# An LSTM with a residual in float32 on one core: weight rows regrouped over 128 partitions, scales per row and chunk, two scalings moved to GpSimd, and wider x products

## The chip, the cores and the metric

The kernel runs on one core of a Trainium2 chip. A core has TensorE (PE, with a weight-load stage shown as PEld), VectorE (DVE), ScalarE (ACT), GpSimd (POOL) and SyncE (SP), each with an instruction queue of its own; they hand work to each other through semaphores. The metric is the device time of one execution in microseconds, the median over several runs. A profile is taken of one execution and has a time of its own.

## The reference

```python
# x: (16, 512, 512), h0: (16, 512), Wx and Wh: (512, 2048), b: (2048,), all float32
xW = einsum('ntd,dg->ntg', x, Wx) + b
def step(carry, xw_t):
    prev_h, prev_c = carry
    a = xw_t + prev_h @ Wh
    i, f, o = sigmoid(a[:, :H]), sigmoid(a[:, H:2*H]), sigmoid(a[:, 2*H:3*H])
    g = tanh(a[:, 3*H:])
    next_c = f * prev_c + i * g
    next_h = o * tanh(next_c)
    return (next_h, next_c), next_h
hs = scan(step, (h0, zeros), xW over time)
return x + hs                       # (16, 512, 512)
```

N = 16 sequences, T = 512 steps, D = H = 512 inputs and units. Each step needs the state of the step before it, so 512 steps follow one another; the products x @ Wx don't depend on the state. The function's arguments are called x, cond_1024 (the h0 above), L0_cond_Wx, L0_cond_Wh and L0_cond_b in the profile.

## The kernel before

**Layout.** The 128 partitions are 4 blocks `j` of 32 (`NJ = 4`, `Q = 32`). For gate sums, block `j` holds the units 128j to 128j+127 along the free axis, and its 32 partitions are rows: 16 sequences twice. Inputs come in pairs of steps (`S2 = 2`, index `q` or `p`), eight steps to a load (`XB = 8`, index `s`, `load_xs`, L138). The DVE's transpose works in squares of 32 x 32, so it turns a gate tile with sequences on partitions into one with units on partitions: partition 32j + k then holds the units 128j + 32c + k for the four chunks `c`. The rows of the weights lie the same way: `load_w` copies, for chunk `c` and block `j`, 32 rows from 128j + 32c on (16 transfers of 256 KB for each of Wh and Wx). The 512 units are treated in two halves, a and b (`h` = 0 and 1, chunks 0, 1 and 2, 3), so that one half's products can run while the other half's elementwise work does.

**Float32 products from float16 parts.** Wh is multiplied by a power of two and split once, at the start, into three float16 parts `wq[0..2]`: the rounded value (L381, ACT), the residual `r1` (L383, DVE) rounded (L384, ACT), and the residual of that, `r2` (L386, DVE), times 4096 (L387, ACT); eight halves of chunks, in `split`. The power of two comes from the largest absolute value of a partition over all four chunks (L360 reduces, L363 to L375 small operations on one column). S is its scale for the output gate, RS and RS2 those for the weights, RSL what undoes S. All of Wh must have landed before the first split, as the scale comes from all of it.

The state is split too: `p1` (L276) writes the rounded product os * tanh(c) into a slot of `parts`, `h` (L270) the float32 value to `hist`, `copy` (L280, ACT), `p2` (L282), `rem` (L286) and `p2r` (L290) the other slots. `os` is the output gate times S (`scale`, L258, ACT: a column as scale).

**One step on PE.** The order is written out in a string. Each `qikh` is a group of eight products (128 x 256, float16) of part `i`, the state's half `k` and the gates' half `h`; four blocks `j` run side by side in the array's columns. Three parts by four combinations make 96 products (`products`, L180). Behind them come `x0` to `x3`, 32 float32 products of 256 columns (`project`, L157), which make the x products two pairs ahead. `seed` (L167, ACT) writes the x sum into a gates bank before a step's products add to it. The first step uses float32 Wh itself (`first_products`, L193).

```python
STEP_PE = "q3aa q3ab q1ab q1aa q2aa q3ba q1ba q2ba q2bb q1bb q2ab q3bb x0 x1 x2 x3"
```

**One step elsewhere.** The order of the elementwise operations is written out too, and no scheduler changes it:

```python
STEP = (
    "turn_a turno_a fold_a tanh_a foldo_a sig_a turn_b sigo_a scale_a mix_a fold_b "
    "tanh_b cell_a ctanh_a turno_b foldo_b sig_b p1_a sigo_b h_a copy_a mix_b p2_a "
    "scale_b cell_b rem_a ctanh_b p2r_a p1_b h_b copy_b p2_b rem_b p2r_b"
)
```

`turn` and `turno` (L216, DVE) transpose a half's gates out of PSUM, `fold` and `foldo` (L223, DVE) add the low-order rows divided by 4096 to the high-order ones, `tanh` (L250), `sig` (L252), `sigo` (L256) and `ctanh` (L268) are ACT's functions, `mix` (L260, one operation for f * c and i * g) and `cell` (L266) DVE's. A step's last operation, `p2r_b`, completes the state's half b, which `q2ba` and `q2bb` of the next step need. In step 0, p1 also waits for memsets of `parts` on POOL.

Every second step ACT undoes the scale for the output (`unscale`, L299: 128 x 128), DVE turns it (L308), POOL adds x (L309), and every eight steps SP issues eight stores (L315) and eight loads of x. Intermediate tiles of a step have two buffers (`work`, `state`), so that an operation writes where that of two steps ago wrote.

**The start.** SP issues the 16 loads of Wh, four of h0, eight of x, then 16 of Wx; ACT's queue issues the bias. Then the scales, the eight splits, the x products of four steps and the seeds; the eight PSUM banks are zeroed by products of a float32 zero row.

## Time and profile before

| | |
|---|---|
| median of 3 runs | 2321.29 us (2321.03 to 2322.24) |
| the profiled execution | 2319.52 us |
| its span | 2317.7 us |
| granted TensorE clock | 0.997 of full speed |
| instructions | 153,753 |
| DMA | 52.13 MB, 22 GB/s on average |
| Wh's loads: issue to landing | 7.6 us (median of 16) |
| Wx's loads: issue to landing | 8.7 us (median of 16) |

The page lists, for each engine, busy time, its share of the span and the number of instructions. Its chain follows the work that ended last back from the end, step by step to what released each instruction, and gives shares by engine. The windows give the same busy figures for a chosen stretch, with the number of instructions in brackets. The timeline has one instruction to a line: start in us, duration in us, engine, line, operation, what it writes and reads with shapes (partitions x elements), and a count. The listing of events has, for each, its duration in ns and its start. A group's row in the list of costly groups has the busy time, the mean duration of one in ns, and the idle time of the engine before them with what ended most of it; PE's groups show durations with overlap in them.

### The profile page before, as it was taken

To read this page: it belongs to the slowest core of one execution; us is meant where nothing else is said; L and a number is where in the kernel's file an instruction comes from. 1 tells how busy PE (TensorE), PEld (TensorE's weight loads), DVE (VectorE), ACT (ScalarE), POOL (GpSimd) and SP (SyncE) were. 2 spreads that over 40 slices of the span, in tenths; PEclk is the share of its full clock that TensorE was granted. 3 is DMA by queue.
4 is the path that set the end of the run, shared out by engine and by line. 5 is a ranking of instruction groups with operands and counts; after the bars stand their busy time and mean duration, and the time that the engine had idled before them with its cause. 6 is when DMAs were issued, how large, how long until landed. Compare 5 with 4: busy or idle time off the path is not lost.

```text
span 2317.7 us, 153753 instructions
## 1 busy us (share of the span) xinstructions
PE 2263.9 (98%) x65584; PEld 1862.2 (80%) x65584; DVE 1958.8 (85%) x11808; ACT 1791.7 (77%) x7704; POOL 117.6 (5%) x264
## 2 busy tenths in 40 slices
PE   4899999999999999999999999999999999999997
PEld 1788888888888888888888888888888888888886
DVE  4788888888888888888888888888888888888887
ACT  3777777777777777777777777777777777777776
POOL 0000000000000000000000000000000000000000
PEclk9999999999999999999999999999999999999999
DMA  7000000000000000000000000000000000000000
GB/s 164 8 18 23 16 20 23 16 20 22 14 22 23 13 23 22 13 23 22 13 22 21 15 23 18 17 23 18 18 22 18 18 23 15 21 23 15 21 18 13
DMA packets 84907, 52.13 MB, mean 22 GB/s; under 512 B 17088, under 2 KB 83200, under 8 KB 83200
## 3 DMA queue, kind: packets, MB, share of 16 engines
q1 hardware_dynamic: 83584, 42.04, 7.9%
q8 instruction: 516, 8.45, 1.6%
q14 instruction: 167, 1.37, 0.2%
q10 hardware_dynamic: 640, 0.26, 0.1%
HBM read 25.46 MB, written 16.78 MB: 18 GB/s over the span
## 4 chain that ended last, share of the span: by engine, by line
PE 96%; DVE 1%; DMA 1%; ACT 1%; issue 0%; ACTq 0%; SPq 0%; POOLq 0%; POOL 0%; DVEq 0%
PE gates L180 58%; PE xb L157 38%; DMA wh_sb<-in_L_cond_Wh_dram 1%; DVE r L383 0%; ACT wq L381 0%; ACT wq L387 0%; PE gates L193 0%; ACT wq L384 0%; DMA bias<-in_L_cond_b_dram 0%; ACTq L334 0%; DVE gt L216 0%; DMA xs<-in_x_dram 0%; SPq L138 0%; DVE r L386 0%; ACT xb L147 0%
## 5 line engine op out<-in xcount | busy, mean ns | idle before, releaser
L180 PE MATMUL gates<-wq,parts 128*32 128x256 f16 x49056 | 1452.1, 273 | 5.3 <-DVE parts L276 4.2
L180 PEld LDWEIGHTS <-parts 128*32 128x32 f16 x49056 | 1306.3, 96 | 155.3 <-DVE parts L276 5.8
L157 PE MATMUL xb<-wx_sb,xT 128*32 128x256 f32 x16384 | 987.0, 380 | 27.1 <-DMA wx_sb<-in_L_cond_Wx_dram 27.1
L157 PEld LDWEIGHTS xb<-wx_sb,xT 128*32 128x32 f32 x16384 | 554.0, 110 | 270.3 <-ACT wq L381 20.2
L216 DVE STREAM_TRANSPOSE gt<-gates 128x192 f32<-128x192 f32 x1024 | 392.1, 383 | 237.0 <-PE gates L180 176.2
L250 ACT ACTIVATE gc<-pre 128x32 f32<-128x32 f32 x1022 | 235.0, 230 | 327.8 <-DVE pre L223 314.8
L167 ACT ACTIVATE gates<-xb,mask 128x256 f32<-128x256 f32 x1024 | 451.5, 441 | 0.0
L258 ACT ACTIVATE os<-so,sc 128x32 f32<-128x32 f32 x1024 | 329.1, 321 | 16.7
L280 ACT COPY parts<-parts 128x32 f16<-128x32 f16 x1022 | 214.5, 210 | 132.1 <-DVE parts L276 132.1
L223 DVE SCALAR_TENSOR_TENSOR pre<-gt 128x96 f32<-128x96 f32 x1024 | 254.2, 248 | 0.0
L252 ACT ACTIVATE sif<-pre 128x64 f32<-128x64 f32 x1024 | 245.5, 240 | 0.0
L216 DVE STREAM_TRANSPOSE gto<-gates 128x64 f32<-128x64 f32 x1024 | 230.3, 225 | 0.0
L309 POOL TENSOR_TENSOR ob<-hb,xs 128x128 f32<-128x128 f32 x256 | 116.6, 456 | 2193.6 <-DVE hb L308 1927.7
L256 ACT ACTIVATE so<-preo 128x32 f32<-128x32 f32 x1024 | 226.7, 221 | 0.0
L290 DVE SCALAR_TENSOR_TENSOR parts<-rem,parts 128x32 f16<-128x32 f32 x1022 | 196.6, 192 | 35.5
L268 ACT ACTIVATE tch<-gc 128x32 f32<-128x32 f32 x1024 | 226.3, 221 | 0.1
L223 DVE SCALAR_TENSOR_TENSOR preo<-gto 128x32 f32<-128x32 f32 x1024 | 193.0, 188 | 17.5
L282 DVE SCALAR_TENSOR_TENSOR parts<-parts,hist 128x32 f16<-128x32 f16 x1022 | 192.8, 189 | 17.7
L260 DVE TENSOR_TENSOR pr<-sif,gc 128x64 f32<-128x64 f32 x1022 | 205.6, 201 | 0.0
L276 DVE TENSOR_TENSOR parts<-os,tch 128x32 f16<-128x32 f32 x1022 | 196.7, 192 | 0.0
L266 DVE TENSOR_TENSOR gc<-pr 128x32 f32<-128x32 f32 x1024 | 192.9, 188 | 0.0
L270 DVE SCALAR_TENSOR_TENSOR hist<-os,tch 128x32 f32<-128x32 f32 x1024 | 189.6, 185 | 0.3 <-ACT tch L268 0.3
(42 smaller groups left out, 685.4 us busy)
## 6 DMA issues: line engine op xcount, KB each, us to landing
xs<-in_x_dram SPq DMA_DIRECT2D x512, 32.0 KB, 2.6
out_dram<-ob SPq DMA_DIRECT2D x512, 32.0 KB, 2.5
wh_sb<-in_L_cond_Wh_dram SPq DMA_DIRECT2D x16, 256.0 KB, 7.6
wx_sb<-in_L_cond_Wx_dram SPq DMA_DIRECT2D x16, 256.0 KB, 8.7
bias<-in_L_cond_b_dram ACTq DMA_DIRECT2D x8, 32.0 KB, 3.3
h_in<-in_cond_dram SPq DMA_DIRECT2D x4, 8.0 KB, 6.9
```

The lines of the kernel that those rows point to most:

```text
L157: nc.tensor.matmul(xb[q % NXB][j * Q : (j + 1) * Q, (1 - e) * GU : (2 - e) * GU], lhsT=xT[q][:, c], rhs=wx_j[:, c, e, j], start=False, sto ...
L167: nc.scalar.mul(gates[h][t % 2][:, :GU].rearrange("p (g u) -> p g u", g=G), xb[t // 2 % NXB].rearrange("p (g h u) -> p h g u", g=G, h=2)[: ...
L180: nc.tensor.matmul(g[j * Q : (j + 1) * Q, :GU], lhsT=a[:, cc, k * N : (k + 2) * N], rhs=wq_j[i - 1][:, 2 * kh + cc, h, j], start=False, st ...
L216: nc.vector.transpose(gt.rearrange("p b m -> p (b m)"), gates[h][t % 2][:, b0 * Q : b1 * Q])
L223: nc.vector.scalar_tensor_tensor(pre.rearrange("p g (c n) -> p (g c) n", c=2), gt[:, :, (1 - t % 2) * N : (2 - t % 2) * N], 1.0 / LO, gt[: ...
L250: nc.scalar.activation(gc[h][:, 0], v["pre", h][:, 0], AF.Tanh)
L252: nc.scalar.activation(new("sif", t, h, [P, 2, 2 * N]), v["pre", h][:, 1:3], AF.Sigmoid)
L256: nc.scalar.activation(new("so", t, h, [P, 2 * N]), v["preo", h][:, 0], AF.Sigmoid)
L258: nc.scalar.mul(new("os", t, h, [P, 2 * N]), v["so", h], S)
L260: nc.vector.tensor_tensor(new("pr", t, h, [P, 2, 2 * N]), v["sif", h], gc[h], ALU.mult)
L268: nc.scalar.activation(new("tch", t, h, [P, 2 * N]), gc[h][:, 1], AF.Tanh)
L280: nc.scalar.copy(slots(t, h, 2), slots(t, h, 0))
```

## The change

The unit on partition p in chunk c becomes 4p + c, where p is the partition of the weights. Each of Wh's chunks is then one transfer over 128 partitions (2,048 columns a row), and Wx comes in eight of 1,024 columns. The transposes of x and h0 read with a step of four elements, the residual's addition reads and writes with one, and so do the splits of Wh, whose parts have the unit's position modulo 4 as an axis; halves a and b of the gates are positions 0, 1 and 2, 3. The gate products read runs of 32 columns in place of 64.

Each partition and chunk gets a scale of its own, from that row of Wh alone (on odd chunks from the sum of the absolute values, an accumulation on ACT; on even ones from the largest, on DVE). So `scales(c)` and the splits of chunk c need only chunk c. The splits are written out as five parts `part(n, k)` in an interleaved order; the last part of every third half moves from ACT to POOL. As the scale now differs by chunk, `scale` is a product with a small tile on POOL, and `unscale` becomes `descale`, a product with a tile on POOL too.

An x product has 512 columns for 256, 16 for 32 in a step. The first loads of x move to ACT's queue, those of h0 and the bias to POOL's; the zero row is float16; the last pair of steps is stored apart from the three before it, on two queues (`put`).

Lines of the changed kernel that the prediction names: L269 `cell`, L279 `p1`, L289 `rem`, L293 `p2r`.

```diff
-STEP_PE = "q3aa q3ab q1ab q1aa q2aa q3ba q1ba q2ba q2bb q1bb q2ab q3bb x0 x1 x2 x3"
+STEP_PE = "q3aa q3ab q1ab q1aa q2aa q3ba q1ba q2ba q2bb q1bb q2ab q3bb x0 x1"
...
-    wq = [const.tile([P, NK, G * H], HP, tag=f"wq{i}", name=f"wq{i}") for i in range(3)]
-    wx_j = wx_sb.rearrange("p c (e g j w) -> p c e j g w", e=2, g=2, j=NJ)
-    wh_j = wh_sb.rearrange("p c (e g j h u) -> p c e h j g u", e=2, g=2, j=NJ, h=2)
-    wq_j = [w.rearrange("p c (g j h u) -> p c h j g u", g=G, j=NJ, h=2) for w in wq]
+    wq = [const.tile([P, NK, NK, G * P], HP, tag=f"wq{i}", name=f"wq{i}") for i in range(3)]
+    wx_j = wx_sb.rearrange("p c (g j w) -> p c j g w", g=G, j=NJ)
+    wh_j = wh_sb.rearrange("p c (e g j u h d) -> p c e h j g d u", e=2, g=2, j=NJ, u=Q, h=2)
+    wq_j = [w.rearrange("p c (h d) (g j u) -> p c h j g d u", h=2, g=G, j=NJ) for w in wq]
...
-    zero = const.tile([1, G * P], FP, tag="zero", name="zero")
+    zero = const.tile([1, G * P], HP, tag="zero", name="zero")
+    ones = const.tile([P, Q], FP, tag="ones", name="ones")
     amax = const.tile([P, NK], FP, tag="amax", name="amax")
-    top = const.tile([P, 1], FP, tag="top", name="top")
...
-    sc = const.tile([P, 5], FP, tag="sc", name="sc")
-    S, RS, RS2, RSL = (sc[:, i : i + 1] for i in range(4))
+    bits = const.tile([P, NK, 2], FP, tag="bits", name="bits")
+    sc = const.tile([P, NK, 4], FP, tag="sc", name="sc")
+    scale = const.tile([P, NK, N], FP, tag="scale", name="scale")
+    unscale = const.tile([P, NK, Q], FP, tag="unscale", name="unscale")
...
-    def load_w(dst, w, c):
-        for j in range(NJ):
-            r0 = j * P + c * Q
-            nc.sync.dma_start(out=dst[j * Q : (j + 1) * Q, c], in_=w[r0 : r0 + Q])
+    def rows(w):
+        return w.rearrange("(p c) f -> p c f", c=NK)
     xs = {}
-    def load_xs(s):
+    def load_xs(s, dma=nc.sync):
         xs[s] = xsp.tile([P, XP, P], FP, tag="xs", name=f"xs_{s}")
         for j in range(NJ):
             for r in range(S2):
                 p0 = j * Q + r * N
-                nc.sync.dma_start(
+                dma.dma_start(
                     out=xs[s][p0 : p0 + N],
                     in_=x[:, s * XB + r : (s + 1) * XB : S2, j * P : (j + 1) * P],
                 )
...
     def turn_x(q):
         s, i = divmod(q, XP)
         xT[q] = xtp.tile([P, NK, Q], FP, tag="xT", name=f"xT_{q}")
-        nc.vector.transpose(xT[q].rearrange("p c m -> p (c m)"), xs[s][:, i])
-    def project(q, c, e):
+        nc.vector.transpose(xT[q], xs[s][:, i].rearrange("p (u c) -> p c u", c=NK))
+    def project(q, c):
         for j in range(NJ):
             nc.tensor.matmul(
-                xb[q % NXB][j * Q : (j + 1) * Q, (1 - e) * GU : (2 - e) * GU],
+                xb[q % NXB][j * Q : (j + 1) * Q],
                 lhsT=xT[q][:, c],
-                rhs=wx_j[:, c, e, j],
+                rhs=wx_j[:, c, j],
...
     def seed(t, h):
         nc.scalar.mul(
-            gates[h][t % 2][:, :GU].rearrange("p (g u) -> p g u", g=G),
-            xb[t // 2 % NXB].rearrange("p (g h u) -> p h g u", g=G, h=2)[:, h],
+            gates[h][t % 2][:, :GU].rearrange("p (g d u) -> p g d u", g=G, d=2),
+            xb[t // 2 % NXB].rearrange("p (g u h d) -> p h g d u", g=G, h=2, d=2)[:, h],
             mask[:, t % 2 : t % 2 + 1],
         )
...
         elif op == "scale":
-            nc.scalar.mul(new("os", t, h, [P, 2 * N]), v["so", h], S)
+            nc.gpsimd.tensor_tensor(
+                two(new("os", t, h, [P, 2 * N])),
+                two(v["so", h]),
+                scale[:, 2 * h : 2 * h + 2],
+                ALU.mult,
+            )
...
-    def unscale(p):
-        hs[p] = work.tile([P, P], FP, tag="hs", name=f"hs_{p}")
-        nc.scalar.mul(
-            hs[p], hist[p // XP][:, p % XP].rearrange("p c m -> p (c m)"), RSL
-        )
+    def descale(p):
+        hs[p] = work.tile([P, NK, Q], FP, tag="hs", name=f"hs_{p}")
+        nc.gpsimd.tensor_tensor(hs[p], hist[p // XP][:, p % XP], unscale, ALU.mult)
+    def put(s, i0, i1, dmas):
+        for j in range(NJ):
+            for r in range(S2):
+                p0 = j * Q + r * N
+                dmas[r % len(dmas)].dma_start(
+                    out=out[:, s * XB + S2 * i0 + r : s * XB + S2 * i1 : S2, j * P : (j + 1) * P],
+                    in_=ob[s][p0 : p0 + N, i0:i1],
+                )
     def residual(p):
         s, i = divmod(p, XP)
         if i == 0:
             ob[s] = outp.tile([P, XP, P], FP, tag="ob", name=f"ob_{s}")
         hb = work.tile([P, P], FP, tag="hb", name=f"hb_{p}")
-        nc.vector.transpose(hb, hs[p])
-        nc.gpsimd.tensor_tensor(ob[s][:, i], hb, xs[s][:, i], ALU.add)
-        if i < XP - 1:
-            return
...
+        nc.gpsimd.tensor_tensor(
+            ob[s][:, i].rearrange("p (u c) -> p u c", c=NK),
+            hb.rearrange("p (c u) -> p u c", c=NK),
+            xs[s][:, i].rearrange("p (u c) -> p u c", c=NK),
+            ALU.add,
+        )
+        if p == NP - 1:
+            put(s, i, i + 1, [nc.sync, nc.scalar])
+        elif p == NP - 2:
+            put(s, 0, i + 1, [nc.sync])
+        elif i == XP - 1:
+            put(s, 0, XP, [nc.sync])
...
-    nc.vector.memset(zero, 0.0)
+    for c in range(NK):
+        nc.sync.dma_start(out=wh_sb[:, c], in_=rows(wh)[:, c])
+    load_xs(0, nc.scalar)
     nc.vector.memset(h_in, 0.0)
-    for c in range(NK):
-        load_w(wh_sb, wh, c)
     for j in range(NJ):
-        nc.sync.dma_start(out=h_in[j * Q : j * Q + N], in_=h0[:, j * P : (j + 1) * P])
-    load_xs(0)
+        nc.gpsimd.dma_start(out=h_in[j * Q : j * Q + N], in_=h0[:, j * P : (j + 1) * P])
     b_j = b.rearrange("(o e g j w) -> j e o g w", o=1, e=2, g=2, j=NJ)
     for j in range(NJ):
         for e in range(2):
-            nc.scalar.dma_start(
+            nc.gpsimd.dma_start(
                 out=bias[j * Q : (j + 1) * Q, (1 - e) * GU : (2 - e) * GU].rearrange(
                     "p (g w) -> p g w", g=2
                 ),
                 in_=b_j[j, e].broadcast_to([Q, 2, P]),
             )
     for c in range(NK):
-        load_w(wx_sb, wx, c)
+        for e in range(2):
+            nc.sync.dma_start(
+                out=wx_sb[:, c, (1 - e) * GH : (2 - e) * GH],
+                in_=rows(wx)[:, c, e * GH : (e + 1) * GH],
+            )
     load_xs(1)
+    nc.vector.memset(zero, 0.0)
+    nc.vector.memset(ones, 1.0)
...
-    nc.scalar.activation(warm, zero[:, 0:1], AF.Sigmoid)
+    nc.scalar.activation(warm, ones[0:1, 0:1], AF.Sigmoid)
...
-    for c in range(NK):
-        nc.vector.tensor_reduce(
-            amax[:, c : c + 1], wh_sb[:, c], mybir.AxisListType.X, ALU.max, apply_absolute_value=True
+    def scales(c):
+        top = amax[:, c : c + 1]
+        if c % 2:
+            junk = tmp.tile([P, G * H], HP, tag="junk", name=f"junk_{c}", bufs=1)
+            nc.scalar.activation(junk, wh_sb[:, c], AF.Abs, accum_out=top)
+        else:
+            nc.vector.tensor_reduce(
+                top, wh_sb[:, c], mybir.AxisListType.X, ALU.max, apply_absolute_value=True
+            )
+        e, inv = bits[:, c, 0:1], bits[:, c, 1:2]
+        S, RS, RS2, RSL = (sc[:, c, i : i + 1] for i in range(4))
+        nc.vector.tensor_scalar(
+            inv.bitcast(I32), top.bitcast(I32), EXP, EXP, ALU.bitwise_and, ALU.bitwise_xor
         )
-    nc.vector.tensor_reduce(top, amax, mybir.AxisListType.X, ALU.max)
-    nc.vector.tensor_scalar(
-        bits[:, 0:1].bitcast(I32), top.bitcast(I32), EXP, None, ALU.bitwise_and
-    )
-    nc.vector.tensor_scalar(
-        bits[:, 1:2].bitcast(I32), top.bitcast(I32), EXP, EXP, ALU.bitwise_and, ALU.bitwise_xor
-    )
-    nc.vector.tensor_scalar(sc[:, 4:5], bits[:, 1:2], 2.0**13, 1.0, ALU.mult, ALU.min)
...
-    def split(c, e):
...
-    nc.vector.transpose(hT0.rearrange("p c m -> p (c m)"), h_in)
+        nc.vector.tensor_scalar(e.bitcast(I32), top.bitcast(I32), EXP, None, ALU.bitwise_and)
+        nc.vector.tensor_scalar(RS2, inv, 2.0**12, 0.5, ALU.mult, ALU.min)
+        nc.vector.tensor_scalar(RS, inv, 2.0**13, 1.0, ALU.mult, ALU.min)
+        nc.vector.tensor_scalar(S, e, 2.0**-14, 1.0, ALU.mult, ALU.max)
+        nc.vector.tensor_scalar(RSL, RS, 1.0 / LO, None, ALU.mult)
+        nc.gpsimd.tensor_scalar(scale[:, c], ones[:, :N], S, None, ALU.mult)
+        nc.gpsimd.tensor_scalar(unscale[:, c], ones, RSL, None, ALU.mult)
+    r1, r2 = {}, {}
+    def part(n, k):
+        c, e = divmod(n, 2)
+        w = wh_sb[:, c, e * GH : (e + 1) * GH].rearrange("p (a d) -> p d a", d=NK)
+        f = [q[:, c, :, (1 - e) * GU : (2 - e) * GU] for q in wq]
+        RS, RS2 = sc[:, c, 1:2], sc[:, c, 2:3]
+        if k == 0:
+            nc.scalar.mul(f[0], w, RS2)
+        elif k == 1:
+            r1[n] = tmp.tile([P, NK, GU], FP, tag="r1", name=f"r1_{n}")
+            nc.vector.scalar_tensor_tensor(r1[n], w, RS, f[0], ALU.mult, ALU.subtract)
+        elif k == 2:
+            nc.scalar.copy(f[1], r1[n])
+        elif k == 3:
+            r2[n] = tmp.tile([P, NK, GU], FP, tag="r2", name=f"r2_{n}")
+            nc.vector.tensor_tensor(r2[n], r1[n], f[1], ALU.subtract)
+        elif n % 3 == 2:
+            nc.gpsimd.tensor_scalar(f[2], r2[n], LO, None, ALU.mult)
+        else:
+            nc.scalar.mul(f[2], r2[n], LO)
     for q in range(2):
         turn_x(q)
-    last = None
+    scales(0)
+    part(0, 0)
+    part(0, 1)
+    nc.vector.transpose(hT0, h_in.rearrange("p (u c) -> p c u", c=NK))
+    for q in range(2):
+        put_bias(q)
+    for n in range(2 * NK):
+        if n % 2 and n + 1 < 2 * NK:
+            scales((n + 1) // 2)
+        if n + 1 < 2 * NK:
+            part(n + 1, 0)
+        part(n, 2)
+        if n + 1 < 2 * NK:
+            part(n + 1, 1)
+        part(n, 3)
+        part(n, 4)
     for c in range(NK):
-        for e in range(2):
-            todo = split(c, e)
-            if last:
-                last()
-            last = todo
-            if (c, e) == (0, 0):
-                for q in range(2):
-                    put_bias(q)
-    last()
-    for q in range(2):
-        for c in range(NK):
-            for e in range(2):
-                project(q, c, e)
+        for q in range(2):
+            project(q, c)
     for t in range(2):
         for h in range(2):
             seed(t, h)
...
         for op in STEP_PE.split():
             if op[0] == "x":
-                i = int(op[1:])
                 if q < NP:
-                    project(q, 2 * half + i // 2, i % 2)
+                    project(q, 2 * half + int(op[1:]))
             elif t:
                 products(t, int(op[1]), "ab".index(op[2]), "ab".index(op[3]))
             elif op[1] == "3":
...
         if t + 2 < T:
             seed(t + 2, 0)
         if t % 2:
-            unscale(t // 2)
+            descale(t // 2)
             if q + 1 < NP:
                 turn_x(q + 1)
         else:
```

## The prediction

> **What bounds the kernel now.** I read the page's busy shares, then its chain, then the windows, and last the timeline of single steps. The page says TensorE:
>
> ```profile
> PE 2263.9 (98%) x65584; PEld 1862.2 (80%) x65584; DVE 1958.8 (85%) x11808; ACT 1791.7 (77%) x7704; POOL 117.6 (5%) x264
> ...
> PE 96%; DVE 1%; DMA 1%; ACT 1%; issue 0%; ACTq 0%; SPq 0%; POOLq 0%; POOL 0%; DVEq 0%
> ```
>
> The windows say otherwise. The first holds two steps of mid-loop; the second about one of the last steps, which have no x products left.
>
> ```profile
> core 0: us, PE busy (x) PEld busy (x) DVE busy (x) ACT busy (x) POOL busy (x), PEclk, DMA share, GB/s
> 996.00:1004.72 8.72, 8.72 (x264) 7.17 (x260) 7.60 (x48) 6.90 (x31) 0.46 (x1) 1.00 0.03 6
> 2300.00:2304.40 4.40, 2.98 (x96) 2.32 (x96) 3.57 (x24) 3.38 (x16) 0.00 (x0) 1.00 0.00 0
> ```
>
> Without its 32 x products PE is busy 2.98 us of a step, and the step still takes 4.36 (products start at 2300.75 and 2305.11). So the step is set by a loop through PE, DVE and ACT, and the x products only fill it. In the single matmul records 24 groups of four f16 products take 109 ns each and 8 groups of x products 216 ns: 4.34 us of PE work in a median step of 4.362. The PE stands 0.02 us below the loop, a coincidence that hides which of the two decides.
>
> The loop in one step, from half b's turn to its last part:
>
> ```profile
> 1003.15 0.38 DVE L216 STREAM_TRANSPOSE gt<-gates 128x192 f32<-128x192 f32 x1
> ...
> 1003.57 0.26 DVE L223 SCALAR_TENSOR_TENSOR pre<-gt 128x96 f32<-128x96 f32 x1
> ...
> 1003.86 0.23 ACT L250 ACTIVATE gc<-pre 128x32 f32<-128x32 f32 x1
> 1004.00 0.21 ACT L268 ACTIVATE tch<-gc 128x32 f32<-128x32 f32 x1
> ...
> 1004.24 0.19 DVE L276 TENSOR_TENSOR parts<-os,tch 128x32 f16<-128x32 f32 x1
> ...
> 1004.71 0.19 DVE L266 TENSOR_TENSOR gc<-pr 128x32 f32<-128x32 f32 x1
> ...
> 1004.93 0.23 ACT L268 ACTIVATE tch<-gc 128x32 f32<-128x32 f32 x1
> ...
> 1005.19 0.19 DVE L276 TENSOR_TENSOR parts<-os,tch 128x32 f16<-128x32 f32 x1
> ...
> 1005.85 0.19 DVE L290 SCALAR_TENSOR_TENSOR parts<-rem,parts 128x32 f16<-128x32 f32 x1
> ```
>
> Read ends against starts: fold_b ends 1003.83 and tanh_b starts 0.03 later; ctanh_a follows tanh_b at ACT's issue distance of 0.135; p1_a starts 0.03 after ctanh_a ends, then mix_b, cell_b, ctanh_b, p1_b, the parts. From turn_b to the start of p2r_b is 2.70 us; its 0.19, 0.15 to q2ba, ten groups of products (1.00) and 0.32 until turn_b can read the gates make 4.36. Each nanosecond on these hand-overs returns in 511 steps.
>
> **The change, part by part.**
>
> *Waits.* An instruction carries one semaphore wait; a second stands before it as an EVENT_SEMAPHORE, and the engine's sequencer decodes the instruction only after that. The profile has this case at p1, in step 0 alone, where p1 also waits for POOL's memsets:
>
> ```profile
> L276 DVEq EVENT_SEMAPHORE  x2: 21/21/21, 72.4 to 73.4; - x2
> ```
>
> ```profile
> 71.29 0.38 DVE L216 STREAM_TRANSPOSE gt<-gates 128x192 f32<-128x192 f32 x1
> ...
> 72.13 0.21 ACT L268 ACTIVATE tch<-gc 128x32 f32<-128x32 f32 x1
> ...
> 72.45 0.19 DVE L276 TENSOR_TENSOR parts<-os,tch 128x32 f16<-128x32 f32 x1
> ...
> 74.13 0.20 DVE L290 SCALAR_TENSOR_TENSOR parts<-rem,parts 128x32 f16<-128x32 f32 x1
> ```
>
> There ctanh to p1 takes 0.10 us instead of 0.03, and turn_b to p2r_b 2.84 instead of 2.70: 0.14 us for two, 69 ns each. In the changed program every p1 waits for ACT (tch) and POOL (os), with the late ACT wait on the EVENT_SEMAPHORE: 1,032 DVE instructions with two waits, 5 before. And on ACT, where the removed scale was the only instruction to wait on ACT's own semaphore and so covered for the rest, tanh, sigo, ctanh and the seeds now carry that wait (sigo one on POOL) beside the old one: 4,083 instructions with two waits, 1 before. The own wait points two steps back and is always met, but the late DVE wait was moved to the EVENT_SEMAPHORE. ACT's one-semaphore events take 17 ns, DVE's 21, so I scale 69 x 17/21 = 56 ns; the least is the 17 ns itself, the most DVE's 69. On the loop lie tanh_b, ctanh_b and two p1. ctanh_a is held by tanh_b + 0.135 (1004.05) later than by cell_a + 0.09 (1004.02), so its event hides. Sum: 2 x 69 + 2 x 56 = 250 ns a step (172 to 276), x 511 = +127.8 us (+88 to +141). Queued behind each waiting instruction is the rest of that engine's step, and the weight load of q2ba waits for its end. The two seed events and sigo's cost nothing: ACT idles 0.48 to 0.71 us before tanh_a.
>
> *Scale and descale on POOL.* ACT loses two L258 (321 ns) a step and an hs (390) every second: worth nothing, as ctanh_b starts 0.03 after cell_b anyway. os_a can start 0.08 after sigo_a (POOL's distance behind hb), at 1003.57; p1_a needs it at 1004.24, with the events at 1004.37. Its price lies between a quarter of the 456 ns of L309 (four times the elements) and all of it: done by 1004.03, hidden; os_b (1004.71 to 1005.17, needed 1005.44) too. What covers descale and the reordered residual is a POOL idle 2,193 us.
>
> *POOL beside DVE.* 183 of the turns of gates ran beside L309 at the same 383 ns, but a turn has one PSUM input. No DVE operation with two SBUF inputs, as nearly all others on the loop are, ever overlapped a POOL one here. Floor 0; ceiling, if each POOL operation pushes the loop back for its whole length, 2 x 0.114 + 0.456/2 = 0.456 us a step. I take 0.06, half of one os, near the floor where the only rows are: +31 us (0 to +233). The Trainium skill speaks against this part: "SBUF — State Buffer", "Who interferes with whom", says that a VectorE instruction with two SBUF inputs and a GpSimd instruction that reads SBUF exclude each other for a whole instruction. By that rule the ceiling would be the better guess, some +202 us on my sum; by the turn rows, -31.
>
> *x products.* 16 of 512 columns for 32 of 256 save one overhead per group: 216 - 213 = 2.5 ns x 4 = 10 ns a step of PE. On a PE that is no longer the limit: 0 (at most -5 us). Products read 32-element runs instead of 64; ten groups lie on the loop, unknown, taken as 0.
>
> *Start.* Before: L381 starts at 28.24, after the whole of Wh; the last L387 ends at 65.00, first products 65.38. After: chunk 0 lands about 10.9 (as the first four loads here; then 4.65 us per MB). Reduce 2.29 and scalars 1.1 (27.24 to 28.24 before) put the first split at 14.5. ACT's order is p0 of the next half (1.15), p2 (1.04), then p4 (1.05), which waits for DVE's p3 (1.23): 4.47 a half, 3.3 where POOL does p4. Six and two make 33.4; the scales of chunks 1 and 3 add 3.1 each (Abs, some 2.0 by L381's rate, and scalars), chunk 2's 3.5, bias copies 1.1, hand-overs 1: ready at 60, so -5 us. The order wins less than landing early promises, since loads end at 25 and the split is what lasts. wx is in by 43, hidden. Faster loads would bring 3 more. L381 and L383 now read Wh with a step of four elements; no row shows that, and doubling these 16 adds 17. Range -8 to +12. The same page's section on the DMA port swizzle notes 16-byte lines, with a penalty for each new one; every such read is a new line, so by that rule the start would be nearer +12.
>
> *End.* Eight stores issue 0.47 apart on SP; four each on two queues save 1.8. POOL's descale for ACT's 0.40: +0.1. Together -1.7.
>
> **Sum.** The profiled execution took 2319.5 (span 2317.7, 1.8 around it), 1.8 below the median 2321.3. 2319.5 + 127.8 + 31 - 5 - 1.7 = 2471.6; say 2472, or 2473 on the median's footing.
>
> **Rivals.**
> - *The split waits cost nothing* (faster): if they passed before the late semaphore, or the PE really set the step, the loop keeps 4.36 and start and end leave 2319.5 - 6.7 = 2313. For it: 98% PE. Against: step 0 at p1, and the last steps. It decides if the events and collisions together stay under 6.7/511 = 13 ns a step. 7%.
> - *POOL and DVE exclude each other* on the loop, at 0.3 us a step instead of 0.06: 2319.5 + 127.8 + 153 - 6.7 = 2594. For it: the DVE's bursts leave hardly a gap. Against: POOL can wait, os has 0.3 us and more to spare. 25%.
> - *ACT's events are cheap*: 17 ns each, no collisions: 2319.5 + 88 - 6.7 = 2401. For it: no ACT event in the trace ends on a late semaphore with ACT idle behind it. 15%.
>
> **How the numbers follow.** Forecast 50%, rivals 25, 15 and 7; the remaining 3 near no change. 0.2% (4.6 us) is what a measurement tells from none. Slower 0.90, same 0.03, faster 0.07. The range, 2385 to 2620, takes in cheap events (2401) and heavy collisions (2594) and leaves out the faster case.
>
> **What would show it.** Right: a median step near 4.67; EVENT_SEMAPHORE some 8 per step on ACT and 2 on DVE; L279's start 0.10 after tch's end; fold_b to tanh_b 0.09 instead of 0.03; PE idle before q2ba, below 95% busy. Collisions: DVE durations of L269, L289 or L293 above 190, or their starts late beside a POOL row. First products near 60. Wrong: a step of 4.36 with the events present, or first products beyond 78.

## The result, and the profile after

The changed kernel takes 2581.39 us (median of 5 runs, 2581.35 to 2581.43); the kernel before takes 2321.29 us beside it. The ratio is 1.1119, with a 95% interval of 1.1103 to 1.1136. That lies in the predicted range (2385 to 2620), 109 us above the predicted 2472: the loss is 260 us where 150 were forecast.

The first view is the page of the changed kernel: busy times of the engines, then the chain by engine and by line.

```profile
PE 2427.2 (94%) x57384; PEld 1382.5 (54%) x57384; DVE 2169.2 (84%) x11822; ACT 1490.0 (58%) x6426; POOL 590.0 (23%) x1566
...
PE 58%; DVE 25%; ACT 12%; issue 5%; DMA 0%; DVEq 0%; ACTq 0%; POOLq 0%; POOL 0%
```

PE is no longer nearly the whole of the chain: DVE, ACT and "issue" (time in which the engine waited for nothing that the profile shows) hold 42% of it. The windows answer to the two shown of before. The first holds two steps of mid-loop, the second one of the last steps, without x products.

```profile
core 0: us, PE busy (x) PEld busy (x) DVE busy (x) ACT busy (x) POOL busy (x), PEclk, DMA share, GB/s
996.00:1005.70 9.70, 9.39 (x232) 5.39 (x230) 8.30 (x48) 5.67 (x27) 2.22 (x6) 1.00 0.01 3
2566.00:2570.72 4.72, 3.12 (x105) 2.19 (x97) 3.98 (x24) 1.87 (x10) 1.15 (x3) 1.00 0.01 3
```

An even and an odd step together take 9.71 us where two steps took 8.72, at the same granted clock of 1.00. In the last step PE is busy for 3.12 of 4.72 us, and the step is no shorter for it: half b's turns start at 2566.44 and 2571.16. Next is the timeline of half b of one odd step of the changed kernel (start and duration in us), with GpSimd's work among it.

```profile
999.16 0.38 DVE L214 STREAM_TRANSPOSE gt<-gates 128x192 f32<-128x192 f32 x1
...
999.61 0.25 DVE L221 SCALAR_TENSOR_TENSOR pre<-gt 128x96 f32<-128x96 f32 x1
999.64 0.34 POOL L256 TENSOR_TENSOR os<-so,scale 128x32 f32<-128x32 f32 x1 [1.12 <-ACT so L254]
999.78 0.24 DVE L269 TENSOR_TENSOR gc<-pr 128x32 f32<-128x32 f32 x1
...
999.96 0.23 ACT L248 ACTIVATE gc<-pre 128x32 f32<-128x32 f32 x1 [0.40 <-DVE pre L221]
1000.12 0.23 ACT L271 ACTIVATE tch<-gc 128x32 f32<-128x32 f32 x1
...
1000.45 0.19 DVE L279 TENSOR_TENSOR parts<-os,tch 128x32 f16<-128x32 f32 x1
...
1000.81 0.28 POOL L256 TENSOR_TENSOR os<-so,scale 128x32 f32<-128x32 f32 x1 [0.84 <-ACT so L254]
1000.91 0.23 DVE L269 TENSOR_TENSOR gc<-pr 128x32 f32<-128x32 f32 x1
...
1001.24 0.23 ACT L271 ACTIVATE tch<-gc 128x32 f32<-128x32 f32 x1 [0.34 <-DVE gc L269]
...
1001.57 0.19 DVE L279 TENSOR_TENSOR parts<-os,tch 128x32 f16<-128x32 f32 x1
...
1001.94 0.47 POOL L302 TENSOR_TENSOR hs<-hist,unscale 128x128 f32<-128x128 f32 x1 [0.85 <-DVE hist L273]
1002.01 0.45 DVE L289 SCALAR_TENSOR_TENSOR rem<-parts,hist 128x32 f32<-128x32 f16 x1
1002.49 0.19 DVE L293 SCALAR_TENSOR_TENSOR parts<-rem,parts 128x32 f16<-128x32 f32 x1
```

Two things are to be seen. First, the gaps: fold_b ends at 999.86 and tanh_b starts 0.10 later, ctanh_b ends at 1001.47 and p1_b starts 0.10 later; before, these gaps were 0.03. Second, the pairs of a POOL row and the DVE row behind it. Both cell rows and rem_b start after POOL's instruction and end 0.04 to 0.05 us after it does: cell_a at 1000.02 (POOL 999.98), cell_b at 1001.14 (1001.09), rem_b at 1002.46 (1002.41). rem_b lasts 0.45 us instead of 0.18.

From medians over 230 steps of each parity, the way from turn_b to p2r_b grew from 2.70 to 3.06 us in even steps and to 3.33 us in the odd steps, which have a descale. The return from p2r_b's end to the next turn_b, which is PE's part, is 1.469 us in both kernels.

| stretch of the loop (start to start, ns) | before | after | of which a second wait | of which beside POOL |
|---|---|---|---|---|
| turn_b to fold_b | 418 | 448 | 30 | |
| fold_b to tanh_b | 292 | 345 | 53 | |
| tanh_b to ctanh_a | 137 | 159 | | 22 (cell_a 57 longer) |
| ctanh_a to p1_a | 245 | 332 | 71 | 16 (ctanh_a no longer follows directly on tanh_b) |
| p1_a to cell_b | 464 | 464 | | |
| cell_b to ctanh_b | 226 | 323 | 60 | 37 (cell_b 34 longer) |
| ctanh_b to p1_b | 262 | 332 | 70 | |
| p1_b to p2r_b, even steps | 658 | 657 | | |
| p1_b to p2r_b, odd steps | 658 | 922 | | 265 |

In the two kernels without os, where POOL does nothing in the loop, tanh_b to ctanh_a is 136 ns with the second waits too, which puts its 22 ns and ctanh_a's 16 into the last column. These 38 ns come from os and a second wait together: cell_a, held until 1000.02, and ctanh_a's own event behind it put ctanh_a at 1000.12; with the 0.03 us of before it could have started at 1000.05, and tanh_b would have let it go at 1000.10. So a step has 284 ns of second waits and 75 ns of os beside DVE, and every other step 265 ns of descale: medians of 4.721 and 4.989 us for 4.362. How the columns were told apart is shown by the experiments. The event rows of the changed kernel, from the views of the three lines (duration in ns, then first and last start):

```profile
L279 DVEq EVENT_SEMAPHORE  x1022: 21/21/21, 78.9 to 2568.8; - x171
...
L248 ACTq EVENT_SEMAPHORE  x1020: 17/17/17, 87.0 to 2571.9; - x170
...
L271 ACTq EVENT_SEMAPHORE  x1020: 17/17/17, 88.1 to 2573.0; - x170
```

The traces show that the late semaphore is the event's. By medians over 440 steps the event starts 31 ns (tanh and ctanh, on ACT) and 37 ns (p1, on DVE) after the end of the late producer, where before the instruction itself started 32 to 34 ns after it; now the instruction follows 45 ns behind the event's end. So the hand-over takes 93 ns to tanh and ctanh and 103 ns to p1, and an event of 17 or 21 ns costs 60 or 70. (At tanh_b the stretch grows by 53 only, as fold_b is 6 ns shorter.)

The two spans differ by 261.6 us. The start takes 6.6 of it (turn_b of the second step at 82.39 for 75.79), 510 steps of 4.880 us for 4.377 on average take 256.4, and the end is 1.4 shorter (8.10 us from the last turn_b for 9.53).

### The profile page after: what moved, and what is told of

Same layout as the page of the kernel before. It is cut to its first block, busy times and chain, and to the rows that moved or that the text cites. A ratio compares the mean times of both kernels' runs of the same rounds, so it can differ in the third digit from the quotient of the medians.

```text
span 2579.3 us, 142464 instructions
## 1 busy us (share of the span) xinstructions
PE 2427.2 (94%) x57384; PEld 1382.5 (54%) x57384; DVE 2169.2 (84%) x11822; ACT 1490.0 (58%) x6426; POOL 590.0 (23%) x1566
## 4 chain that ended last, share of the span: by engine, by line
PE 58%; DVE 25%; ACT 12%; issue 5%; DMA 0%; DVEq 0%; ACTq 0%; POOLq 0%; POOL 0%
PE gates L178 42%; PE xb L155 15%; ACT gates L165 8%; DVE gt L214 4%; DVE parts L279 4%; DVE gc L269 3%; DVE pr L263 3%; ACT tch L271 2%; DVE preo L221 2%; DVE pre L221 2%; DVE gto L214 2%; DVE parts L285 1%; DVE hist L273 1%; DVE rem L289 1%; ACT wq L408 1%
## 5 line engine op out<-in xcount | busy, mean ns | idle before, releaser
L178 PE MATMUL gates<-wq,parts 128*32 128x256 f16 x49056 | 1601.3, 274 | 87.0 <-ACT gates L165 70.3
L178 PEld LDWEIGHTS <-parts 128*32 128x32 f16 x49056 | 1120.2, 96 | 819.7 <-DVE parts L279 406.4
L155 PE MATMUL xb<-wx_sb,xT 128*32 128x512 f32 x8192 | 976.7, 593 | 15.1 <-DMA wx_sb<-in_L_cond_Wx_dram 15.1
L256 POOL TENSOR_TENSOR os<-so,scale 128x32 f32<-128x32 f32 x1024 | 320.1, 313 | 1297.0 <-ACT so L254 1295.5
L155 PEld LDWEIGHTS xb<-wx_sb,xT 128*32 128x32 f32 x8192 | 262.3, 110 | 322.2 <-issue 321.4
L165 ACT ACTIVATE gates<-xb,mask 128x256 f32<-128x256 f32 x1024 | 434.3, 443 | 0.5
L279 DVE TENSOR_TENSOR parts<-os,tch 128x32 f16<-128x32 f32 x1022 | 196.9, 193 | 76.2 <-ACT tch L271 6.7
L289 DVE SCALAR_TENSOR_TENSOR rem<-parts,hist 128x32 f32<-128x32 f16 x1022 | 252.2, 247 | 0.0
L269 DVE TENSOR_TENSOR gc<-pr 128x32 f32<-128x32 f32 x1024 | 239.5, 234 | 0.0
L319 POOL TENSOR_TENSOR ob<-hb,xs 128x128 f32<-128x128 f32 x256 | 133.1, 520 | 418.2 <-DVE hb L318 340.4
L263 DVE TENSOR_TENSOR pr<-sif,gc 128x64 f32<-128x64 f32 x1022 | 226.2, 221 | 2.0 <-ACT sif L250 0.8
L293 DVE SCALAR_TENSOR_TENSOR parts<-rem,parts 128x32 f16<-128x32 f32 x1022 | 196.5, 192 | 35.3
```

The costliest lines, as they stand in the source:

```text
L155: nc.tensor.matmul(xb[q % NXB][j * Q : (j + 1) * Q], lhsT=xT[q][:, c], rhs=wx_j[:, c, j], start=False, stop=(c == NK - 1), skip_group_chec ...
L165: nc.scalar.mul(gates[h][t % 2][:, :GU].rearrange("p (g d u) -> p g d u", g=G, d=2), xb[t // 2 % NXB].rearrange("p (g u h d) -> p h g d u" ...
L178: nc.tensor.matmul(g[j * Q : (j + 1) * Q, :GU], lhsT=a[:, cc, k * N : (k + 2) * N], rhs=wq_j[i - 1][:, 2 * kh + cc, h, j], start=False, st ...
L256: nc.gpsimd.tensor_tensor(two(new("os", t, h, [P, 2 * N])), two(v["so", h]), scale[:, 2 * h : 2 * h + 2], ALU.mult,)
L263: nc.vector.tensor_tensor(new("pr", t, h, [P, 2, 2 * N]), v["sif", h], gc[h], ALU.mult)
L269: nc.vector.tensor_tensor(gc[h][:, 1], pr[:, 0], pr[:, 1], ALU.add)
```

## The experiments

**Only os on GpSimd.** The kernel before with one operation moved:

```diff
-            nc.scalar.mul(new("os", t, h, [P, 2 * N]), v["so", h], S)
+            nc.gpsimd.tensor_tensor(
+                new("os", t, h, [P, 2 * N]), v["so", h], scale, ALU.mult
+            )
```

> The kernel before with one edit: os = so * S is made by GpSimd with a tile that holds S, everything else stays. This brings the second waits on p1 (DVE) and on tanh, ctanh and sigo (ACT), and GpSimd's work beside DVE's. Theory (in the changed kernel's even steps the loop is 0.36 us longer: 0.26 from four split waits, 0.10 from os beside DVE): both parities at 4.72, 2321 + 511 x 0.36 = 2505 us. Rival 1 (waits are nearly free, the loss is GpSimd against DVE and mostly descale): 0.10 a step, 2372. Rival 2 (the loss lies in the new layout, not in this move): 2321.

2510.69 us, ratio 1.0813 (1.0797 to 1.0829): 189 us slower. The median step is 4.726 and 4.722 us by parity, and each stretch of the table above is within 6 ns of the changed kernel's even steps. This move alone, in the old layout, makes the whole of the even steps' loss; rivals 1 and 2 are out.

**Only descale on GpSimd.**

```diff
-        nc.scalar.mul(
-            hs[p], hist[p // XP][:, p % XP].rearrange("p c m -> p (c m)"), RSL
+        nc.gpsimd.tensor_tensor(
+            hs[p], hist[p // XP][:, p % XP].rearrange("p c m -> p (c m)"), undo, ALU.mult
         )
```

> The kernel before with one edit: unscale of the output is a product with a tile on GpSimd instead of ACT, every second step. No instruction on the loop gets a second wait. Theory (descale shuts rem_b out for its length, 0.26 us in the steps that have one): odd steps 4.62, even ones 4.36, 2321 + 256 x 0.26 = 2388 us. Rival (GpSimd and DVE run beside each other, the long odd steps come from something else): 2321.

2356.76 us, ratio 1.0149 (1.0134 to 1.0164): 35 us slower, half of what the theory expected, as each odd step loses 0.14 us and not 0.26. Even steps stay at 4.363, odd ones take 4.504. The timeline of this kernel shows why it is half:

```profile
1004.41 0.50 POOL L301 TENSOR_TENSOR hs<-hist,undo 128x128 f32<-128x128 f32 x1 [3.19 <-DVE hist L272]
1004.41 0.18 DVE L288 SCALAR_TENSOR_TENSOR rem<-parts,hist 128x32 f32<-128x32 f16 x1
1004.63 0.33 DVE L292 SCALAR_TENSOR_TENSOR parts<-rem,parts 128x32 f16<-128x32 f32 x1
```

Here rem_b starts together with descale and gets through in 0.18; p2r_b comes next and is held until 0.05 after descale's end, 0.33 for 0.19. Descale itself takes 0.50 us, where it takes 0.46 with no such DVE instruction beside it (in the kernel that holds it back, below). In the changed kernel descale starts 0.07 ahead of rem_b, and rem_b pays. The price depends on which instruction is met, and how early in POOL's work.

**Without os: second waits on ACT with no work on GpSimd.** p1 and h take so and a column with S (p1 is shown):

```diff
-            nc.vector.tensor_tensor(
-                slots(t, h, 0), two(v["os", h]), two(v["tch", h]), ALU.mult
+            nc.vector.scalar_tensor_tensor(
+                slots(t, h, 0), two(v["so", h]), S, two(v["tch", h]), ALU.mult, ALU.mult
```

> The kernel before without the operation os: p1 and h take so, the column S (or S x 4096) and tch in one instruction of DVE. GpSimd gets nothing to do. The one instruction of ACT that waited for ACT itself is gone, so tanh, ctanh, sigo and the seeds get a second wait. Theory (an ACT wait split off costs 60 ns where the late semaphore is on it): tanh_b and ctanh_b on the loop, 2 x 60 = 0.12 us a step, 2321 + 61 = 2382 us, up to 2400 if the later sig also holds up mix_a and with it fold_b. Rival (split waits are free, only GpSimd costs): 2321 or a little less.

**The same with one copy on ACT that takes the waits over.**

```diff
+        elif op == "own":
+            nc.scalar.copy(seen[:, 0:1], v["so", h][:, 0:1])
...
-    "scale_b cell_b rem_a ctanh_b p2r_a p1_b h_b copy_b p2_b rem_b p2r_b"
+    "cell_b rem_a ctanh_b p2r_a p1_b h_b copy_b own_b p2_b rem_b p2r_b"
```

> As the one without os, and at the end of every step ACT copies one column of so_b to a column nobody reads: this instruction waits for ACT itself, so that tanh, ctanh, sigo and the seeds are left with one wait. Theory: the step is back at 4.36, 2321 us, though ACT does more than without the copy. Rival (not the second waits, but the fused p1 and h cost the time): the same as without the copy, 2382 to 2400.

2516.05 us (ratio 1.0836, 1.0817 to 1.0854) without the copy and 2438.41 us (1.0502, 1.0487 to 1.0518) with it. Both expectations of the totals missed, and each named theory was half right. The rival's claim, that the fused operations cost the time, holds for most of it: against the kernel before, the version with the copy is still 0.246 us a step longer. The row of the fused p1 of the first of the two kernels says where:

```profile
L277 DVE SCALAR_TENSOR_TENSOR parts<-so,sc,tch 128x32 f16<-128x32 f32 x1022 | 257.2, 252 | 19.0 <-ACT tch L269 4.2
```

It takes 252 ns where p1 with two tiles took 192, and h 246 for 185; both stand on the loop in both halves, 4 x 60 = 0.24 us. But the difference between the two versions is what was wanted: the same operations, POOL idle in both, and one instruction more for ACT in the faster one. In the traces ACT has 4,095 EVENT_SEMAPHOREs without the copy and 15 with it, as many as in the kernel before. Adding the copy takes 77.6 us off, 0.15 a step. The median step goes from 4.750 to 4.608, and the 142 ns lie at fold_b (29), tanh_b (53) and ctanh_b (60). So second waits on ACT cost time by themselves. The 29 ns at fold_b come from sig_a, which follows the late tanh_a: it ends 60 ns later, so that mix_a gets its input 1,180 ns after turn_a's start, just when mix_a starts in both versions; mix_a then ends 40 ns later, and fold_b behind it starts 29 later. The changed kernel has the same 1,180 and 40.

**The changed kernel with its second waits taken over.**

```diff
...
+        elif op == "own":
+            nc.scalar.copy(seen[:, 0:1], v["so", h][:, 0:1])
+        elif op == "seen":
+            nc.vector.tensor_scalar(
+                seen[:, 1 + h : 2 + h], v["os", h][:, 0:1], 1.0, None, ALU.mult
```

> The changed kernel with three small instructions a step that take the second waits over where nobody is late: ACT copies one column of so_b after copy_b (waits for ACT itself), and DVE reads one column of os_a ahead of foldo_b and of os_b ahead of p2r_a (wait for GpSimd). p1, tanh, ctanh and the seeds are left with one wait; GpSimd's work stays. Theory (in the even steps 0.29 of the 0.36 us come from split waits: fold_b 0.03 through sig, tanh_b 0.05, p1_a 0.07, ctanh_b 0.06, p1_b 0.07): 2581 - 511 x 0.29 = 2435 us. Rival (GpSimd's work beside DVE holds the same places up, waits or not): little change, 2540 to 2581.

2444.37 us, ratio to the kernel before 1.0531 (1.0515 to 1.0546): 137 us less than the changed kernel, by three instructions more a step. The gaps before tanh_b, p1_a and ctanh_b are back at 0.03 us; p1_b's is 0.06, as it now stands behind p2r_a and the read of os_b. A part of the gain is lost again at another place, as the timeline of this kernel shows:

```profile
1000.49 0.25 POOL L257 TENSOR_TENSOR os<-so,scale 128x32 f32<-128x32 f32 x1 [2.15 <-ACT so L255]
1000.50 0.35 DVE L222 SCALAR_TENSOR_TENSOR pre<-gt 128x96 f32<-128x96 f32 x1
```

os_a now comes 60 ns earlier, and starts just ahead of fold_b instead of just behind it. fold_b, 96 elements wide, takes 0.35 us for 0.26, where cell_a had been held before. That is 0.10 us where os beside DVE had cost 0.075 in all.

**The changed kernel with descale held back.** GpSimd first reads a column that p2r_b has written:

```diff
+            if t + 1 < T:
+                nc.gpsimd.tensor_scalar(
+                    late[:, t // 2 % 2 : t // 2 % 2 + 1],
+                    slots(t, 1, 3)[:, 1, N - 1 : N],
+                    1.0,
+                    None,
+                    ALU.mult,
+                )
             descale(t // 2)
```

> The changed kernel with GpSimd held up ahead of descale by a read of one column that p2r_b has written, so that descale runs after the step's last DVE instruction on the loop and not beside rem_b; no work is removed, one small one added. Theory (descale shuts rem_b out of SBUF for 0.265 us in the odd steps): odd steps fall from 4.99 to 4.73, 2581 - 256 x 0.265 = 2513 us. Rival (the odd steps are long because turn_x reads with a step of four, or because GpSimd is the bound in them): 2581 or more.

2514.38 us, 67 less than the changed kernel; the odd steps take 4.721 for 4.989, the even ones stay at 4.725. In the timeline of this kernel rem_b is back at 0.18, and descale runs at its old length where nobody on the loop meets it:

```profile
1005.92 0.18 DVE L290 SCALAR_TENSOR_TENSOR rem<-parts,hist 128x32 f32<-128x32 f16 x1
1006.14 0.19 DVE L294 SCALAR_TENSOR_TENSOR parts<-rem,parts 128x32 f16<-128x32 f32 x1
1006.42 0.21 POOL L473 TENSOR_SCALAR late<-parts 128x1 f16<-128x1 f16 x1 [1.67 <-DVE parts L294]
1006.59 0.46 POOL L303 TENSOR_TENSOR hs<-hist,unscale 128x128 f32<-128x128 f32 x1
```

**Both edits together.** The two edits are combined:

```diff
+        elif op == "own":
+            nc.scalar.copy(seen[:, 0:1], v["so", h][:, 0:1])
...
+                nc.gpsimd.tensor_scalar(
+                    late[:, t // 2 % 2 : t // 2 % 2 + 1],
...
```

> Both edits in one: the second waits taken over, descale held up until p2r_b. Theory: the two causes lie at different places of the loop and add up, 2581 - 146 - 68 = 2367 us, with 0.07 a step left of os beside DVE. Rival (they share a cover, so that the second brings less): 2400 or more.

2376.11 us, ratio 1.0239 (1.0223 to 1.0254). The two gains are 137 and 67, together 205.3: they add up, so they lie at different places of the loop. The steps take 4.480 and 4.475, 0.12 and 0.11 above the kernel before: 0.10 at fold_b beside os_a, the rest at p1_b behind the read of os_b.

**The changed kernel with both scalings back on ACT.** Both take one column of chunk 0 for all chunks, so the factors by chunk are left out.

```diff
-            nc.gpsimd.tensor_tensor(
-                two(new("os", t, h, [P, 2 * N])),
-                two(v["so", h]),
-                scale[:, 2 * h : 2 * h + 2],
-                ALU.mult,
-            )
+            nc.scalar.mul(new("os", t, h, [P, 2 * N]), v["so", h], sc[:, 0, 0:1])
...
-        nc.gpsimd.tensor_tensor(hs[p], hist[p // XP][:, p % XP], unscale, ALU.mult)
+        nc.scalar.mul(hs[p], hist[p // XP][:, p % XP], sc[:, 0, 3:4])
```

> The changed kernel with scale and descale back on ACT, each with one column of chunk 0 for all chunks (the per-chunk factors are left out). All the rest stays: the layout 4p + c, products that read runs of 32 columns, x products of 512 columns, the reordered start and residual. Theory (the loop's loss is all in the two moves to GpSimd): step 4.36 as before, start 6 later, end 1.4 earlier, 2321 + 4 = 2326 us. Rival (runs of 32 columns, strided transposes or the residual cost something in the loop): 10 us more for each 20 ns of a step.

2320.49 us, ratio 0.9998 (0.9988 to 1.0008). The median step is 4.366 for 4.362, the mean 4.370 for 4.377. Everything else that the change does, the layout, the runs of 32 columns, the reordered transposes and the residual with its stride on GpSimd, costs nothing that shows in the loop. The loop's whole loss is in the two moves. The total comes out equal: the start, still 6.5 us late at the second step, is nearly made up by the shorter mean step and the earlier end.

**The changed kernel with the splits of Wh read in memory order.** The reordering of Wh's columns is left out, so this kernel doesn't compute the LSTM; its instructions and sizes are the same.

```diff
-        w = wh_sb[:, c, e * GH : (e + 1) * GH].rearrange("p (a d) -> p d a", d=NK)
+        w = wh_sb[:, c, e * GH : (e + 1) * GH].rearrange("p (d a) -> p d a", d=NK)
```

> The changed kernel with the splits of Wh read in memory order instead of with a step of four elements (the reordering of Wh's columns is left out; all instructions, sizes and orders stay). Theory (the strided reads cost L408 2.09 us for 1.13 and L411 2.04 for 1.28, eight times each, some of it side by side): first products 8 to 13 us earlier, at 57 to 62 us, total 2568 to 2573. Rival (the interleaved order and the scales by chunk, not the stride, make the start late): first products stay at 70, 2581.

2569.71 us, 11.7 less than the changed kernel at the same mean step of 4.880, and the first products start at 57.9 us for 70.1 (65.4 in the kernel before). The two groups of costly instructions that the edit touches, first with the stride of four elements (the changed kernel), then without (mean of one in ns after the bar, behind the busy time):

```profile
L408 ACT ACTIVATE wq<-wh_sb,sc 128x1024 f16<-128x1024 f32 x8 | 16.9, 2109 | 12.9 <-DVE sc L392 12.9
L411 DVE SCALAR_TENSOR_TENSOR r<-wh_sb,sc,wq 128x1024 f32<-128x1024 f32 x8 | 16.4, 2046 | 14.7 <-ACT wq L408 14.7
```

```profile
L411 DVE SCALAR_TENSOR_TENSOR r<-wh_sb,sc,wq 128x1024 f32<-128x1024 f32 x8 | 10.3, 1284 | 8.7 <-ACT wq L408 8.7
L408 ACT ACTIVATE wq<-wh_sb,sc 128x1024 f16<-128x1024 f32 x8 | 9.1, 1142 | 12.2 <-DVE sc L392 12.2
```

The stride makes the ACT read 1.85 times and the DVE read 1.6 times as long. The new start is 7.5 us earlier than the old one without the stride; the stride takes 12.2 back.

**Only the wider x products**, in the kernel before.

```diff
-                xb[q % NXB][j * Q : (j + 1) * Q, (1 - e) * GU : (2 - e) * GU],
+                xb[q % NXB][j * Q : (j + 1) * Q],
...
-                rhs=wx_j[:, c, e, j],
+                rhs=wx_j[:, c, j],
```

> The kernel before with x products of 512 columns, 16 a step for 32 (Wx is loaded with its halves swapped, in 32 transfers for 16); nothing else. Theory (the loop sets the step, but PE stands 0.02 us below it and is late in some steps: mean step 4.378 against a median of 4.362; 10 ns less PE work a step takes a part of these away): 2316 to 2319 us. Rival (PE work never shows): 2321.

2315.33 us; the kernel before took 2318.64 beside this run and the next two. The ratio is 0.9984 (0.9975 to 0.9992): 3.3 us less. The median step is not shorter (4.365 for 4.362); the mean is (4.369 for 4.377), since of 497 steps 3 instead of 22 took more than 4.5 us. PE does show, in the steps where it falls behind.

**Only the ends: the interleaved splits without a stride, and the last stores on two queues**, in the kernel before.

```diff
+    part(0, 0)
+    part(0, 1)
+    for n in range(2 * NK):
+        if n + 1 < 2 * NK:
+            part(n + 1, 0)
+        part(n, 2)
+        if n + 1 < 2 * NK:
+            part(n + 1, 1)
+        part(n, 3)
+        if n:
+            part(n - 1, 4)
...
+        if p == NP - 1:
+            put(s, i, i + 1, [nc.sync, nc.scalar])
+        elif p == NP - 2:
+            put(s, 0, i + 1, [nc.sync])
```

> The kernel before with two edits at its ends only: the eight splits in the interleaved order of the changed kernel (the next half's first rounding ahead of this half's second, so that ACT doesn't wait for DVE), and the last pair's stores on two queues. Layout, loads, the single scale and the loop stay. Theory (ACT needs 1.13 + 1.05 + 1.05 less three overlaps of 0.09 = 2.95 us a half for 4.4): the last split ends at 54 instead of 65, and the end is 1.5 shorter: 2308 us. Rival (the first step waits for Wx and the x products instead): 2316 to 2320.

2305.06 us, ratio 0.9940 (0.9928 to 0.9952): 13.6 us less. First products at 55.0 for 65.4, the end 7.54 us after the last turn_b for 9.53.

**These ends and the wider x products together.**

```diff
-STEP_PE = "q3aa q3ab q1ab q1aa q2aa q3ba q1ba q2ba q2bb q1bb q2ab q3bb x0 x1 x2 x3"
+STEP_PE = "q3aa q3ab q1ab q1aa q2aa q3ba q1ba q2ba q2bb q1bb q2ab q3bb x0 x1"
...
+        part(n, 2)
+        if n + 1 < 2 * NK:
+            part(n + 1, 1)
```

> The last two together: interleaved splits, stores of the last pair on two queues, and x products of 512 columns. Theory: the gains lie in different stages and add up, 2321 - 12.5 - 4 = 2304 us. Rival: 2308 or more.

2300.41 us, ratio 0.9921 (0.9907 to 0.9934): faster than both kernels, by 18 and 281 us. It keeps the single scale, the old layout and both scalings on ACT. PE's and ACT's share on its page:

```profile
PE 2258.5 (98%) x57392; PEld 1571.4 (68%) x57392; DVE 1958.7 (85%) x11808; ACT 1791.5 (78%) x7704; POOL 117.7 (5%) x264
```

## Why the prediction was right or wrong

**What bounds the kernel: right.** Two causes that touch no PE instruction, second waits and GpSimd's work, moved the step by 0.36 to 0.63 us, and some 10 ns less PE work a step brought 3.3 us in all.

**Waits: right, a little small.** The forecast was 250 ns a step: 69 on each of two p1 and 56 on each of tanh_b and ctanh_b. Measured are 71 and 70 on p1, 53 and 60 on ACT: step 0 of the trace before held DVE's price. ACT's 56 came near by luck: it was scaled by the lengths of the two events, while the greater part of the price, the 45 ns behind the event, is the same on both engines. The forecast left out what the later sig does to mix_a and fold_b, 30 ns. 284 x 511 = 145 us for 127.8. In the changed kernel, taking the waits over brought 137 us, with part of it lost again at fold_b.

**os on GpSimd: right in place, near in size by a guess.** os never made p1 late: it ends 0.47 us before p1 starts in both halves. Its cost is DVE held beside it, 75 ns for the forecast 60. But the 60 stood for all of GpSimd's work beside DVE, and the trace before had no such meeting to take a size from. The prediction also had ctanh_a's event hidden; it is hidden without os (136 ns from tanh_b in the two kernels of that kind), and not behind a held cell_a.

**Descale: the term that failed.** The prediction said that "What covers descale and the reordered residual is a POOL idle 2,193 us". The idle time hid how long descale takes and not what it does to DVE: descale runs in the middle of half b's last DVE operations and holds rem_b for 265 ns in every second step, 256 x 0.265 = 68 us. The prediction had its own bound for that (0.456 / 2 a step) and didn't put a part of it into the sum. The residual, on the same POOL, was rightly costed at nothing: the step that has it is no longer than in the kernel with os alone.

**The rule that was weighed.** By the rows, a DVE instruction with two SBUF inputs that starts behind a GpSimd instruction (by 0.07 to 0.15 us in the rows shown of the changed kernel) ends no earlier than 0.04 to 0.05 us after it; the 96 columns of fold_b, in the kernel with the waits taken over, end 0.11 after it. One that starts ahead keeps its time, and GpSimd is late: os takes 0.34 us where fold_b started ahead of it, for 0.25. Turns with one PSUM input keep their 383 ns (242 of them overlap L309 in the trace before, at 382 to 384). The Trainium skill, "SBUF — State Buffer", "Who interferes with whom", says that such a pair shuts each other out for the whole instruction, and the case's rows agree. The ceiling that the prediction tied to this rule, 202 us on the sum, was still twice too high: 0.21 us a step were lost of 0.456, as an instruction loses only the rest of the other's length, and part of it off the loop.

**x products: right within its bracket.** The prediction took 0 and at most -5 us; measured alone they bring -3.3.

**Start: wrong in sign.** Forecast -5, measured +6.6 at the second step; the first products come at 70.1 us and not at 60. The term that failed was the stride, left at 0 with the remark that doubling these 16 instructions "adds 17": they became 1.85 and 1.6 times as long, and without the stride the first products come 12.2 us earlier. The Trainium skill, "SBUF — State Buffer", in its section on the DMA port swizzle, has 16-byte lines in SBUF with a penalty for every new one; the 2.11 us for 1.14 of these reads agree. The prediction had this at the end of its range and not in its sum. -5 + 12.2 would have been near.

**End: right.** -1.4 for -1.7.

**The sum.** 2471.6, and to it 17 for the waits, 8 for os, 68 for descale and 12 for the start make 2577. Irregular steps make the rest: the mean step stands 0.025 us above the median in the changed kernel and 0.015 before, some 5 us in all. The rival with heavy collisions (2594) came nearer than the forecast (2472): it had the same split waits and 0.3 us a step of collisions, where 0.21 were measured and the forecast had 0.06. So on GpSimd beside DVE, 106 of the 260 us, the rival was nearer the truth, and the result lies in the range because the range took it in; on the waits, 145 us, the forecast was right. Rival 3, cheap ACT events, and the faster case are out by the two kernels without os and by the two with only one move.

## What to carry to other kernels

Where a chain of short hand-overs between engines sets the time, look at what semaphores each instruction on it has to wait for after the change, and which of them is late: moving an operation off an engine can take away the one wait that covered the others, and a tiny instruction off the chain that waits in their place gives the time back (137 us here). Idle time of GpSimd said nothing here of what its work costs VectorE; place such work where no VectorE operation of the chain with two SBUF inputs stands, as the held-back descale did for 67 us. A good order of the start should be tried apart from the layout that came with it: without its strided reads it was worth 10 us.

## What was not expected

- A scalar_tensor_tensor with a column as its scalar took 252 ns on 128 x 32 where the two-tile product took 192, and 246 where the same operation with a constant took 185.
- Taking a wait away moved a collision: os_a, 60 ns earlier, met fold_b instead of cell_a, and the loss beside GpSimd rose from 0.075 to about 0.10 us a step.
- GpSimd is held up too: os took 0.34 us where it met fold_b, and 0.25 where it started ahead of it.
- Why descale met rem_b in the changed kernel and p2r_b in the kernel with descale alone was read from their start times; it was not varied by itself. A place for os on GpSimd where it meets no operation of the loop was not tried.
